# A depthwise 3x3 convolution moved to 64x64 TensorE tiles, with its later steps placed by a table

## The chip, the cores and the metric

The kernel runs on one core of one Trainium2 chip. The time is device microseconds of one execution, the median of several. The engines in the profile are PE (TensorE, matrix products), PEld (its weight loads), DVE (VectorE), ACT (ScalarE), POOL (GpSimd) and SP (SyncE, which starts transfers). All data are 32-bit floats, except for a few throw-away outputs.

## The reference, cut to what matters

The program is four residual layers over `x` of shape (4, 256, 48, 48). Each layer normalises its input in groups of 8 channels (`_gn`), computes something and adds it to `x`. Layer 0 is an 8-head attention, layer 1 a gate from a large depthwise convolution, layer 2 a one-head attention with a batch norm over all four images. The change is in layer 3:

```python
def _L3_conv_ref(x, attn_w1, attn_w2, refine_w, refine_b):
    p = jnp.mean(xw, axis=(2, 3))
    h = jax.nn.leaky_relu(p @ attn_w1.T, SLOPE)
    a = jax.nn.sigmoid(h @ attn_w2.T)
    y = xw * a[:, :, None, None]
    y = jax.lax.conv_general_dilated(y, refine_w, ..., feature_group_count=C)
    y = y + refine_b[None, :, None, None]
    mu = jnp.mean(y, axis=(2, 3), keepdims=True)
    var = jnp.mean(jnp.square(y - mu), axis=(2, 3), keepdims=True)
    y = (y - mu) * jax.lax.rsqrt(var + EPS)
    return jax.nn.leaky_relu(y, SLOPE)
x = x + _L3_conv_ref(_gn(x), ...)
```

So each channel is filtered by its own 3x3 kernel, gets a bias, is normalised over its 48x48 pixels, goes through a leaky ReLU and is added to `x`.

## The kernel before

Channels lie on the 128 partitions, in two halves `k`; pixels lie along the row, 2304 of them, cut into six slices of 384 (eight image rows). A tile of layer 3 is one image and one half of the channels, so there are eight (`TILES`). All engines follow an order written out by hand: each executes its instructions in the order in which the Python code emits them, and waits by semaphores for what the others make.

Layers 0 to 2 run in `attend`, a loop over attention groups into whose slots other work is placed. One such piece of work is `diagonals`, which lies beside the last attention of layer 2: for every tap that PE computes it builds a diagonal matrix of the tap's 128 weights, so that a product with it multiplies each channel by its own weight.

Layer 3 has a head, a loop and a tail. The head closes layer 2's batch norm (`sc2`, `bi2`), checks the softmax sums (`ok`, `okm`, `sound`, read at the very end to choose between this path and a general one), and prepares the first image: `Pre.first` multiplies by `Ww` on PE, ScalarE applies the batch norm, DVE or GpSimd add to `x`, `Pre.stats` and `Pre.chain` compute the group norm and the channel gate, and ScalarE writes the padded 50x50 images (`pads`). For the other images the same work is spread over the loop as `Pre.add`, `Pre.stats` and `Pre.chain`.

The loop runs over 8 tiles and, in each, over 6 slices. For each slice PE computes four of the nine taps (`PE_TAPS`) as 128x128 products into PSUM, one slice per bank (`products`). For each pair of slices DVE adds the five other taps, in place in PSUM, each reading a shifted window of the padded image (`taps`). Then ScalarE adds the bias, writes the result `z` to SBUF and sums it (`evict`). The steps that follow for each tile are `centre` and `square` (sum of squares about a rough mean, ScalarE), `scales` and `shift` (tiny DVE instructions and a GpSimd root), `scale` (ScalarE), `leak` (DVE), `gain` (add to `x`, GpSimd) and `store`. Their places are `if s == ...` lines in the loop, some a tile later, some two. `two_banks` hands out in turn the three PSUM tiles of two banks; a pair of slices takes one.

Of the kernel before, what the change touches and what calls it, by code (L numbers as in the profile page):

```python
# [9 lines left out]
F32 = mybir.dt.float32  # L10
AF = mybir.ActivationFunctionType
ALU = mybir.AluOpType
AX = mybir.AxisListType

P = 128
HW = 48
N = HW * HW
NK = 2
HEADS = 8
D = 64  # L20
NPAIR = HEADS // 2
JB = N // P
SL = 384
NSL = N // SL
# [13 lines left out]
V_BOUT, V_G1, V_B1, V_M1, V_V1, V_WB, V_G2, V_B2, V_RB = range(9)  # L38
# [31 lines left out]
LW = 2 * SL // P  # L70
SUM_HI = 1e25
SUM_LO = 1e-20


def usual_path(
    tc, x, wqkv, wout, vecs, dww, thphi_w, thphi_b, g_w, g_b, W_w, attn_w1, attn_w2, refine_w, out
):
    nc = tc.nc
# [12 lines left out]
    def pj_tile():  # L91
        return ps_pj.tile([P, 512], F32, tag="pj", name="pj")
# [16 lines left out]
    vec = cpool.tile([P, 9, NK], F32, name="vec")  # L109
# [18 lines left out]
    rfw = cpool.tile([P, NK, 9], F32, name="rfw")  # L128
# [5 lines left out]
    ident = cpool.tile([P, P], F32, name="ident")  # L134
# [12 lines left out]
    ones = cpool.tile([P, D], F32, name="ones")  # L147
# [6 lines left out]
    lsum = cpool.tile([P, LW], F32, name="lsum")  # L154
    nc.vector.memset(lsum, 0.0)
    lmin = cpool.tile([P, LW], F32, name="lmin")
# [70 lines left out]
    lp = main.enter_context(tc.tile_pool(name="l1", bufs=1))  # L227

    HALVES = (slice(0, D), slice(D, P))
# [383 lines left out]
    ident2 = lp.tile([P, D], F32, name="ident2")  # L613
# [394 lines left out]
        }  # L1008


    PE_TAPS = (0, 1, 2, 3)
    DVE_TAPS = (4, 5, 6, 7, 8)
    diag = {}

    def diagonals():

        for k in range(NK):
            xs = xsp.tile([P, NK, SL + 1], F32, tag="xs", name="diag")
            xs = xs.rearrange("p k s -> p (k s)")[:, : len(PE_TAPS) * P]
            diag[k] = xs.rearrange("p (t j) -> p t j", j=P)  # L1020
            for n, t in enumerate(PE_TAPS):
                nc.gpsimd.tensor_scalar(
                    diag[k][:, n, :], ident, rfw[:, k, t : t + 1], None, ALU.mult
                )
                yield 1

# [132 lines left out]
    n = NCH * NG  # L1159
    AT_CHUNK = AT_AFTER % NG  # L1160
    for i, (b, p) in enumerate(order):
# [12 lines left out]
        else:  # L1174
            start, slices = project2(0, norms2[0], twos[0])
# [9 lines left out]
        if b > 0:  # L1185
            end = n - 2 if (b, p) == (B - 1, NPAIR - 1) else n + 1
# [9 lines left out]
    n = L2C * NG  # L1196
    for b in range(B):
        work, others = {}, []

        def stats(b, c):  # L1200
            return [lambda k=k: w_stats(b, k, c) for k in range(NK)]
# [4 lines left out]
        if b + 1 < B:  # L1206
            spread(work, stats(b, 0), [22, 23])
            start, slices = project2(b + 1, norms2[b + 1], twos[b + 1])
# [6 lines left out]
            at = [s for s in range(n) if s in work or s % NG == AT_TOTAL]  # L1215
# [3 lines left out]
        else:  # L1219
            spread(work, stats(b, 0), [14, 15])  # L1220
            spread(work, stats(b, 1), [23, 24])
            others.append((diagonals(), NK * len(PE_TAPS), 4, 22))
        phases.append(([l2_unit(b, c, twos[b]) for c in range(L2C)], work, others))
# [34 lines left out]
    lp = l3.enter_context(tc.tile_pool(name="l3", bufs=1))  # L1258
    wk = l3.enter_context(tc.tile_pool(name="l3w", bufs=2))
# [20 lines left out]
    nc.vector.tensor_add(bi2, bi2, vec[:, V_B2, :])  # L1280


    W2 = HW + 2
    NPAD = 4
    pads = [lp.tile([P, W2, W2], F32, tag=f"pad{i}", name=f"pad{i}") for i in range(NPAD)]
    TILES = [(n, k) for n in range(B) for k in range(NK)]
    RS = SL // HW
    NG3 = NSL // 2
    GW = 2 * SL

    def two_banks(n):
        if n % 3 < 2:
            return sc_tile()
        return ps_av.tile([P, 2, 512], F32, tag="av", name="av3")
# [120 lines left out]
    class Conv:  # L1415


        def __init__(self, i):
            self.i, (n, self.k) = i, TILES[i]
            self.b = SEQ[n]  # L1420
            self.pad = pads[i % NPAD]
            self.z = big.tile([P, N], F32, tag="qk"[i // 2 % 2], name="z")

            self.st = small.tile([P, 2, NG3], F32, tag="in_st", name="in_st", bufs=3)
            self.ps = {}

        def products(self, s):
            g = s // 2
            if s % 2 == 0:
                self.ps[g] = two_banks(self.i * NG3 + g)  # L1430
            for n, t in enumerate(PE_TAPS):
                dr, dc = divmod(t, 3)
                nc.tensor.matmul(
                    self.ps[g][:, s % 2, :SL].rearrange("p (r c) -> p r c", c=HW),
                    lhsT=diag[self.k][:, n, :],
                    rhs=self.pad[:, s * RS + dr : (s + 1) * RS + dr, dc : dc + HW],
                    start=n == 0, stop=n == len(PE_TAPS) - 1,
                )

        def taps(self, g):  # L1440
            z = self.ps[g][:, :, :SL].rearrange("p h (r c) -> p h r c", c=HW)
            for t in DVE_TAPS:
                dr, dc = divmod(t, 3)
                r0 = 2 * g * RS + dr
                src = self.pad[:, r0 : r0 + 2 * RS, dc : dc + HW]
                nc.vector.scalar_tensor_tensor(  # L1446
                    z, src.rearrange("p (h r) c -> p h r c", h=2),
                    rfw[:, self.k, t : t + 1], z, ALU.mult, ALU.add,
                )

        def evict(self, g):
            nc.scalar.activation(
                self.z[:, g * GW : (g + 1) * GW].rearrange("p (h s) -> p h s", h=2),
                self.ps[g][:, :, :SL], AF.Identity, bias=vec[:, V_RB, self.k : self.k + 1],
                accum_out=self.st[:, 0, g : g + 1],
            )

        def centre(self):
# [45 lines left out]
    ALL = slice(0, N)  # L1504
    THIRDS = [slice(i * GW, (i + 1) * GW) for i in range(NG3)]
    for i in range(NPAD):
        for e in (0, W2 - 1):
            nc.gpsimd.memset(pads[i][:, e, :], 0.0)
            nc.gpsimd.memset(pads[i][:, 1 : W2 - 1, e : e + 1], 0.0)


    ok = lp.tile([P, 2, LW], F32, name="ok")
    nc.vector.tensor_scalar(ok[:, 0, :], lsum, SUM_HI, None, ALU.is_le)
    nc.vector.tensor_scalar(ok[:, 1, :], lmin, SUM_LO, None, ALU.is_ge)
    okm = lp.tile([P, 1], F32, name="okm")
    nc.vector.tensor_reduce(okm, ok, AX.XY, ALU.min)
    ps = pj_tile()
    nc.tensor.matmul(ps[0:1, 0:1], lhsT=okm, rhs=ones[:, 0:1], start=True, stop=True)
    sound = lp.tile([1, 1], mybir.dt.int32, name="sound")
    nc.vector.tensor_scalar(sound, ps[0:1, 0:1], P - 0.5, None, ALU.is_ge)  # L1520

    pres = {0: Pre(0), 1: Pre(1)}
    for i in range(NK * L2C):
# [12 lines left out]
            steps[NK * (b - 2) + 1, 2 * c] = (b, c)  # L1536
            steps[NK * (b - 1), 2 * c] = (b, L2C + c)

    convs, pending = [], None
    for i, (b, k) in enumerate(TILES):  # L1540
        cv = Conv(i)
        convs.append(cv)
        prev = convs[i - 1] if i else None
        older = convs[i - 2] if i > 1 else None
        final = i == len(TILES) - 1
        rest = iter(())
        for s in range(NSL):

            if pending:
                pending()  # L1550
                pending = None
            if s == 0 and k == 1 and b + 1 < B:
                rest = pres[b + 1].chain()
                next(rest)
            elif s:
                next(rest, None)
            step = steps.get((i, s))
            if step:
                n, at = step
                if n not in pres:  # L1560
                    pres[n] = Pre(n)
                pres[n].add(at)
                pending = lambda n=n, at=at: pres[n].stats(at)
            cv.products(s)
            next(rest, None)
            if s == 0 and prev:
                prev.taps(NG3 - 1)
                prev.evict(NG3 - 1)
            if s == 1 and prev:
                prev.square(NG3 - 1)  # L1570
                prev.scales()
            if s == 2:
                cv.taps(0)
                if prev:
                    prev.shift()
                cv.evict(0)
            if s == 3:
                cv.centre()
                if prev:
                    prev.scale(ALL)  # L1580
            if s == 4:
                cv.taps(1)
                cv.evict(1)
                cv.square(0)
            if s == 5:
                cv.square(1)
                if prev:
                    prev.leak(ALL)
            if older and s % 2:
                older.gain(THIRDS[s // 2], nc.gpsimd)  # L1590
                if s == NSL - 1:
                    older.store(ALL)
        _drain(rest)

    cv, prev = convs[-1], convs[-2]
    g = NG3 - 1
    cv.taps(g)
    cv.evict(g)
    cv.square(g)
    for cols in THIRDS:  # L1600
        prev.gain(cols, nc.gpsimd)
        prev.store(cols)
    cv.scales()
    cv.shift()
    for cols in THIRDS:
        cv.scale(cols)
        cv.leak(cols)
        cv.gain(cols, nc.vector)
        cv.store(cols)
    said = nc.values_load(sound[0:1, 0:1])  # L1610
    strict.close()
    l3.close()
# [843 lines left out]
```

## Time and profile before

| | |
|---|---|
| median time of 3 runs | 3713.06 us (3712.05 to 3713.46) |
| span of the profiled execution | 3710.8 us |
| PE busy | 3522.4 us (95%) |
| DVE busy | 2588.3 us (70%) |
| ACT busy | 2344.5 us (63%) |
| POOL busy | 1444.7 us (39%) |
| first convolution product of layer 3 | at 3480.92 us |
| L1446, the five taps on DVE | 120 instructions of 768 columns, 1.02 us each |
| L1433, the four taps on PE | 384 records of 384 columns |
| L1452, the eviction on ScalarE | 24 instructions, 0.90 us each |

Times inside the profile are microseconds from the start of the span. In a line of the timeline the first number is the start, the second the duration of the group; "x5" is a group of five instructions; the brackets tell how long the engine was idle before and on what it waited. In a table of windows each engine has its busy time and, in brackets, its number of instructions; PEclk is the share of the full TensorE clock that was granted. A product of 32-bit floats appears as two records.

### The profile page before, as it was taken

To read this page: it belongs to the slowest core of one execution; us is meant where nothing else is said; L and a number is where in the kernel's file an instruction comes from. 1 tells how busy PE (TensorE), PEld (TensorE's weight loads), DVE (VectorE), ACT (ScalarE), POOL (GpSimd) and SP (SyncE) were. 2 spreads that over 40 slices of the span, in tenths; PEclk is the share of its full clock that TensorE was granted. 3 is DMA by queue.
4 is the path that set the end of the run, shared out by engine and by line. 5 is a ranking of instruction groups with operands and counts; after the bars stand their busy time and mean duration, and the time that the engine had idled before them with its cause. 6 is when DMAs were issued, how large, how long until landed. Compare 5 with 4: busy or idle time off the path is not lost.

```text
span 3710.8 us, 86538 instructions
## 1 busy us (share of the span) xinstructions
PE 3522.4 (95%) x36330; PEld 1759.4 (47%) x36330; DVE 2588.3 (70%) x3203; ACT 2344.5 (63%) x3819; POOL 1444.7 (39%) x900
## 2 busy tenths in 40 slices
PE   7999999999999999999999999999999998999685
PEld 4444444454444444444444444444444445654343
DVE  2455555476778777967787779767968786576687
ACT  4665666666776677557766775587578555555353
POOL 2333333333334333433343334433433455664242
PEclk9999999999999999999999999999999999999797
DMA  4111111111111111121111111111111100000001
GB/s 138 24 25 21 26 21 26 21 25 21 25 21 26 20 29 17 34 55 34 21 25 21 25 21 25 21 25 21 25 16 25 17 6 6 6 8 4 26 29 74
DMA packets 114591, 97.89 MB, mean 26 GB/s; under 512 B 56224, under 2 KB 111632, under 8 KB 112400
## 3 DMA queue, kind: packets, MB, share of 16 engines
q1 hardware_dynamic: 111728, 91.27, 12.8%
q8 instruction: 286, 4.69, 0.5%
q10 hardware_dynamic: 2464, 1.00, 0.1%
q14 instruction: 113, 0.93, 0.1%
HBM read 59.33 MB, written 11.80 MB: 19 GB/s over the span
## 4 chain that ended last, share of the span: by engine, by line
PE 68%; DVE 18%; issue 5%; ACT 4%; POOL 3%; DMA 2%; SPq 0%; DVEq 0%; ACTq 0%; POOLq 0%
PE av L258 26%; PE sc L238 26%; DVE acc L284 7%; PE pj L512 6%; PE pj L584 3%; PE pj L533 3%; DVE sc L1446 2%; PE pj L291 1%; POOL half L269 1%; ACT pt L244 1%; DVE av L1446 1%; DVE acc L278 1%; PE pj L828 1%; ACT prod L766 1%; DMA xs<-in_x_dram 1%
## 5 line engine op out<-in xcount | busy, mean ns | idle before, releaser
L244 ACT ACTIVATE pt<-sc 128x768 f32<-128x768 f32 x1944 | 1476.5, 812 | 814.1 <-PE sc L238 805.4
L269 POOL TENSOR_TENSOR half<-pt 128x768 f32<-128x768 f32 x477 | 954.1, 2001 | 1673.4 <-ACT pt L244 1611.7
L238 PE MATMUL sc<-q,k 64*64 64x384 f32 x13824 | 1279.6, 485 | 12.7 <-ACT pt L244 9.9
L258 PE MATMUL av<-pt,v 64*64 64x384 f32 x13824 | 1279.8, 485 | 0.0
L284 DVE TENSOR_TENSOR acc<-acc,pt 128x768 f32<-128x768 f32 x792 | 930.7, 1175 | 86.2 <-DVE acc L284 1.8
L238 PEld LDWEIGHTS sc<-q,k 64*64 64x64 f32 x13824 | 510.6, 133 | 638.2 <-issue 499.9
L258 PEld LDWEIGHTS av<-pt,v 64*64 64x64 f32 x13824 | 514.4, 133 | 594.0 <-issue 557.3
L284 DVE TENSOR_TENSOR acc<-acc,half 128x768 f32<-128x768 f32 x459 | 468.6, 1021 | 335.7 <-POOL half L269 334.1
L589 DVE SCALAR_TENSOR_TENSOR x<-pj,bo,x 128x384 f32<-128x384 f32 x192 | 118.0, 615 | 461.9 <-PE pj L584 461.7
L512 PE MATMUL pj<-xs,w 128*128 128x384 f32 (+1 forms) x768 | 298.5, 512 | 3.2 <-issue 1.7
L766 ACT ACTIVATE prod<-pd,wt 128x256 f32<-128x256 f32 x486 | 280.6, 743 | 0.2
L339 POOL TENSOR_TENSOR o<-o,rinv 128x384 f32<-128x384 f32 x95 | 128.9, 1356 | 284.3 <-DMA rinv<-rinv 273.2
L512 PEld LDWEIGHTS pj<-xs,w 128*128 128x128 f32 x768 | 131.0, 190 | 157.3 <-issue 53.9
L584 PE MATMUL pj<-o,wo 128*128 128x384 f32 x384 | 159.8, 501 | 33.3 <-DVE x L589 28.7
L258 PE MATMUL av<-pt,qv 64*64 64x384 f32 x1728 | 173.9, 496 | 0.0
L238 PE MATMUL sc<-qv,kd 64*64 64x384 f32 x1728 | 169.4, 486 | 2.4 <-ACT pt L244 2.4
L784 DVE TENSOR_REDUCE prod<-prod 128x256 f32<-128x1280 f32 x114 | 168.5, 1478 | 0.0
L278 DVE TENSOR_TENSOR acc<-pt 128x768 f32<-128x768 f32 x99 | 139.3, 1407 | 26.4 <-ACT pt L244 26.4
L533 PEld LDWEIGHTS pj<-w,xs 128*128 128x128 f32 x1152 | 143.8, 192 | 26.0 <-issue 0.6
L533 PE MATMUL pj<-w,xs 128*128 128x128 f32 x1152 | 144.1, 275 | 0.0
L518 ACT ACTIVATE k<-pj,bias 128x384 f32<-128x384 f32 x96 | 55.7, 580 | 127.5 <-PE pj L512 127.0
L335 POOL TENSOR_TENSOR o<-raw 128x384 f32<-128x384 f32 x95 | 117.7, 1238 | 0.0
(226 smaller groups left out, 2686.7 us busy)
## 6 DMA issues: line engine op xcount, KB each, us to landing
xs<-in_x_dram SPq DMA_DIRECT2D x96, 384.0 KB
rinv<-rinv SPq DMA_DIRECT2D x208, 94.5 KB
x<-in_x_dram SPq DMA_DIRECT2D x6, 1152.0 KB
out_dram<-x SPq DMA_DIRECT2D x6, 1152.0 KB
l<-row SPq DMA_DIRECT2D x416, 1.5 KB
w<-in_wqkv_dram SPq DMA_DIRECT2D x32, 192.0 KB
rinv<-ls SPq DMA_DIRECT2D x208, 1.5 KB
x_out<-x SPq DMA_DIRECT2D x6, 384.0 KB
```

Source lines behind the costliest of these rows:

```text
L238: nc.tensor.matmul(ps[c * D : (c + 1) * D, h, :SL], lhsT=u["of"]["k"][r, j0 : j0 + D], rhs=u["of"]["q"][r, u["qc"]], start=True, stop=True,)
L244: nc.scalar.activation(pt, ps[:, :, :SL], AF.Exp, scale=u["scale"])
L258: nc.tensor.matmul(u["av"][h * D : (h + 1) * D, half, :SL], lhsT=value(u, j, h)[r], rhs=pt[r, h, :], start=j == 0, stop=j == JB - 1,)
L269: nc.gpsimd.tensor_add(half, pts[0], pts[1])
L278: nc.vector.tensor_add(u["acc"], ready[0], ready[1])
L284: nc.vector.tensor_add(u["acc"], u["acc"], term)
L339: eng.tensor_mul(o, o, u["rinv"])
L512: nc.tensor.matmul(ps[:, :n], lhsT=at["w"][:, k, t, :], rhs=xs[s][:, k, :n], start=k == 0, stop=k == NK - 1,)
L533: nc.tensor.matmul(ps[:, i * P : (i + 1) * P], lhsT=xs[s][:, k, i * P : (i + 1) * P], rhs=at["w"][:, k, 2, :], start=k == 0, stop=k == NK - 1,
L584: nc.tensor.matmul(ps[:, :SL], lhsT=wo[:, p, k * P : (k + 1) * P], rhs=o["o"], start=True, stop=True,)
L766: nc.scalar.activation(bufs[n % 3][:, :, min(n, 1) + i].rearrange("p (r c) -> p r c", c=AS), pd[:, PAD + dr : PAD + dr + AS, PAD + dc : PA ...
L784: nc.vector.tensor_reduce(to, bufs[n % 3][:, :, : min(n, 1) + len(taps)], AX.X, ALU.add)
```

## The change

Three things change. First, the products of layer 3 use 64x64 tiles of TensorE instead of the whole array: a diagonal matrix of 128 channels has only zeros in two of its four quadrants, so each half of the channels (`HALVES`, partitions 0 to 63 and 64 to 127) can be multiplied by itself, and the two other quadrants are free for another tap. Two taps are computed at a time for each half: the first (`e` = 0) goes to the same half of the output, the second (`e` = 1) to the other half. Eight of the nine taps thus go to TensorE.

Second, each half's sum is then in two places. `other` (ScalarE) brings the half that lies on the wrong partitions to the right ones in SBUF, `part`, and adds the bias, for which `rb_x` holds the bias with its halves exchanged. `own` (DVE) adds the ninth tap to the half that lies right and writes `z`. `join` (DVE) adds the two and sums the result. There is one PSUM tile of two banks for each slice now, instead of for each pair.

Third, the steps behind each slice are written as a table: `after` gives for each step its distance in slices from the tile's first and a rank within that slice, and `run` emits what is due. `scale`, `leak` and `gain` go by thirds of a tile. The check of the softmax sums becomes a generator, `judge`, that is advanced in the first tile's slices.

```diff
-    PE_TAPS = (0, 1, 2, 3)
-    DVE_TAPS = (4, 5, 6, 7, 8)
+    PE_TAPS, DVE_TAP = (0, 1, 2, 3, 5, 6, 7, 8), 4
...
-                    diag[k][:, n, :], ident, rfw[:, k, t : t + 1], None, ALU.mult
+                    diag[k][:, n, :], ident2, rfw[:, k, t : t + 1], None, ALU.mult
...
+    rb_x = lp.tile([P, NK], F32, name="rb_x")
+    for to, fr in zip(HALVES, HALVES[::-1]):
+        nc.sync.dma_start(rb_x[to, :], vecs[fr, V_RB, :])
...
         def products(self, s):
+            self.ps[s] = two_banks(self.i * NSL + s)
+            last = len(PE_TAPS) // 2 - 1
+            for n in range(last + 1):
+                for h, r in enumerate(HALVES):
+                    for e in range(2):
+                        nc.tensor.matmul(
+                            self.ps[s][HALVES[h ^ e], h, :SL].rearrange(
+                                "p (r c) -> p r c", c=HW
+                            ),
+                            lhsT=diag[self.k][r, 2 * n + e, :],
+                            rhs=self.window(r, s, PE_TAPS[2 * n + e]),
+                            start=n == 0, stop=n == last,
+                        )
+
+        def other(self, s):
...
+            for h, r in enumerate(HALVES):
+                fr = HALVES[1 - h]
+                nc.scalar.activation(
+                    self.part[g][r, s % 2, :], self.ps[s][fr, h, :SL], AF.Identity,
+                    bias=rb_x[fr, self.k : self.k + 1],
+                )
+
+        def own(self, s):
+            z = self.z[:, s * SL : (s + 1) * SL].rearrange("p (r c) -> p r c", c=HW)
+            for h, r in enumerate(HALVES):
                 nc.vector.scalar_tensor_tensor(
+                    z[r], self.window(r, s, DVE_TAP), rfw[r, self.k, DVE_TAP : DVE_TAP + 1],
+                    self.ps[s][r, h, :SL].rearrange("p (r c) -> p r c", c=HW),
+                    ALU.mult, ALU.add,
+                )
+
+        def join(self, g):
+            z = self.z[:, g * GW : (g + 1) * GW]
+            nc.vector.tensor_tensor_reduce(
+                z, z, self.part[g].rearrange("p h s -> p (h s)"), 1.0, 0.0, ALU.add, ALU.add,
+                self.st[:, 0, g : g + 1],
             )
...
+    def after(cv, final):
+        at = []
+        for s in range(NSL):
+            at += [(s + 1, 0, lambda s=s: cv.own(s)), (s + 1, 0, lambda s=s: cv.other(s))]
+        for g in range(NG3):
+            at.append((2 * g + 3, 1, lambda g=g: cv.join(g)))
+            at.append((2 * g + 4, 3, lambda g=g: cv.square(g)))
+        at.append((3, 1, cv.centre))
+        at += [(9, 2, cv.scales), (10, 2, cv.shift)]
+        eng = nc.vector if final else nc.gpsimd
+        for g, cols in enumerate(THIRDS):
+            at.append((10 + g, 4, lambda cols=cols: cv.scale(cols)))
+            at.append((11 + g, 1, lambda cols=cols: cv.leak(cols)))
+            at.append((12 + g, 5, lambda cols=cols: cv.gain(cols, eng)))
+            if final:
+                at.append((12 + g, 6, lambda cols=cols: cv.store(cols)))
+        if not final:
+            at.append((14, 6, lambda: cv.store(ALL)))
+        return at
```

More of the change, by code (lines that the diff above doesn't have):

```diff
@@ L1018, in diagonals @@
             xs = xsp.tile([P, NK, SL + 1], F32, tag="xs", name="diag")
-            xs = xs.rearrange("p k s -> p (k s)")[:, : len(PE_TAPS) * P]
-            diag[k] = xs.rearrange("p (t j) -> p t j", j=P)
+            xs = xs.rearrange("p k s -> p (k s)")[:, : len(PE_TAPS) * D]
+            diag[k] = xs.rearrange("p (t j) -> p t j", j=D)
             for n, t in enumerate(PE_TAPS):
                 nc.gpsimd.tensor_scalar(
-                    diag[k][:, n, :], ident, rfw[:, k, t : t + 1], None, ALU.mult
+                    diag[k][:, n, :], ident2, rfw[:, k, t : t + 1], None, ALU.mult
                 )
@@ L1424, in __init__, with window @@
             self.st = small.tile([P, 2, NG3], F32, tag="in_st", name="in_st", bufs=3)
-            self.ps = {}
+            self.ps, self.part = {}, {}
+        def window(self, r, s, t):
+            dr, dc = divmod(t, 3)
+            return self.pad[r, s * RS + dr : (s + 1) * RS + dr, dc : dc + HW]
         def products(self, s):
+            self.ps[s] = two_banks(self.i * NSL + s)
[11 more added lines that the diff above has]
+                        )
@@ L1428, in products @@
+        def other(self, s):
             g = s // 2
             if s % 2 == 0:
[L1430 to L1437, printed above, removed]
-                )
@@ L1440, in taps @@
[L1440 to L1445, printed above, removed]
+                self.part[g] = wk.tile([P, 2, SL], F32, tag="part", name="part")
+            for h, r in enumerate(HALVES):
[3 more added lines that the diff above has]
+                    bias=rb_x[fr, self.k : self.k + 1],
+                )
@@ L1446, in taps @@
+        def own(self, s):
+            z = self.z[:, s * SL : (s + 1) * SL].rearrange("p (r c) -> p r c", c=HW)
+            for h, r in enumerate(HALVES):
                 nc.vector.scalar_tensor_tensor(
-                    z, src.rearrange("p (h r) c -> p h r c", h=2),
-                    rfw[:, self.k, t : t + 1], z, ALU.mult, ALU.add,
-                )
[L1451 to L1455, printed above, removed]
+                    z[r], self.window(r, s, DVE_TAP), rfw[r, self.k, DVE_TAP : DVE_TAP + 1],
+                    self.ps[s][r, h, :SL].rearrange("p (r c) -> p r c", c=HW),
+                    ALU.mult, ALU.add,
+                )
@@ L1509, in usual_path, with judge @@
             nc.gpsimd.memset(pads[i][:, 1 : W2 - 1, e : e + 1], 0.0)
[L1512 to L1518, printed above, removed]
-    sound = lp.tile([1, 1], mybir.dt.int32, name="sound")
-    nc.vector.tensor_scalar(sound, ps[0:1, 0:1], P - 0.5, None, ALU.is_ge)
+    sound = lp.tile([1, 1], mybir.dt.int32, name="sound")
+    def judge():
+        ok = lp.tile([P, 2, LW], F32, name="ok")
+        nc.vector.tensor_scalar(ok[:, 0, :], lsum, SUM_HI, None, ALU.is_le)
+        nc.vector.tensor_scalar(ok[:, 1, :], lmin, SUM_LO, None, ALU.is_ge)
+        okm = lp.tile([P, 1], F32, name="okm")
+        nc.vector.tensor_reduce(okm, ok, AX.XY, ALU.min)
+        yield
+        ps = pj_tile()
+        nc.tensor.matmul(ps[0:1, 0:1], lhsT=okm, rhs=ones[:, 0:1], start=True, stop=True)
+        yield
+        nc.vector.tensor_scalar(sound, ps[0:1, 0:1], P - 0.5, None, ALU.is_ge)
+        yield
     pres = {0: Pre(0), 1: Pre(1)}
@@ L1537, in usual_path, with run @@
             steps[NK * (b - 1), 2 * c] = (b, L2C + c)
-    convs, pending = [], None
+    def after(cv, final):
[17 more added lines that the diff above has]
+        return at
+    events = {}
+    def run(t, ranks):
+        now = [(rank, fn) for rank, fn in events.get(t, ()) if rank in ranks]
+        for _, fn in sorted(now, key=lambda job: job[0]):
+            fn()
+    pending, verdict = None, judge()
     for i, (b, k) in enumerate(TILES):
         cv = Conv(i)
[L1542 to L1545, printed above, removed]
+        for dt, rank, fn in after(cv, i == len(TILES) - 1):
+            events.setdefault(i * NSL + dt, []).append((rank, fn))
         rest = iter(())
         for s in range(NSL):
+            t = i * NSL + s
+            run(t, (0,))
             if pending:
@@ L1565, in usual_path @@
             next(rest, None)
[L1566 to L1592, printed above, removed]
-        _drain(rest)
[L1595 to L1609, printed above, removed]
+            if i == 0:
+                next(verdict, None)
+            run(t, range(1, 7))
+        _drain(rest)
+    end = len(TILES) * NSL
+    for t in range(end, end + 9):
+        run(t, range(7))
     said = nc.values_load(sound[0:1, 0:1])
```

## The prediction

> **What bounds the kernel now.** I read the page first and then asked the trace about the last 260 us, where the edited code runs. Part 2 of the page shows PE at 9 tenths for 36 of 40 slices; only the last three slices, layer 3, look different. The windows over layer 3 (head, loop of convolution slices, tail) give its size and its busiest engine:
>
> ```profile
> core 0: us, PE busy (x) PEld busy (x) DVE busy (x) ACT busy (x) POOL busy (x), PEclk, DMA share, GB/s
> 3454.00:3481.00 27.00, 10.96 (x74) 5.42 (x71) 14.95 (x43) 8.55 (x9) 8.10 (x21) 0.63 0.07 30
> 3481.00:3695.00 214.00, 168.26 (x556) 87.05 (x556) 174.78 (x258) 97.61 (x145) 75.42 (x49) 0.88 0.09 37
> 3695.00:3711.00 16.00, 0.00 (x0) 0.00 (x0) 6.59 (x12) 4.88 (x7) 0.73 (x2) 0.50 0.28 108
> ```
>
> The loop is 214 us for 8 tiles, 26.8 us each. DVE is busy 82% of it, PE 79% at a clock of 0.88. The chain of waits inside the loop says which of the two is the limit:
>
> ```profile
> by line: DVE sc L1446 26.3%; DVE av L1446 15.3%; DVE z L1495 9.0%; PE sc L1433 7.6%; issue 7.0%; ACT z L1452 4.5%; DVE gn_st L1345 3.6%; ACT junk L1465 3.3%; POOL x L1340 3.2%; ACT pad L1408 2.0%; ACT tmp L1316 2.0%; POOL x_back L1340 1.6%;
> ```
>
> DVE's taps (L1446) and leak (L1495) are half of it; PE's products only 7.6%. The timeline of a late tile shows the mechanism: five taps run one after another in 5.25 us, ScalarE's eviction waits 6.29 us for them, and PE's next products wait for the eviction.
>
> ```profile
> 3653.25 5.25 DVE L1446 SCALAR_TENSOR_TENSOR sc<-pad,rfw,sc 128x768 f32<-128x768 f32 x5
> ...
> 3658.59 0.90 ACT L1452 ACTIVATE z<-sc,vec 128x768 f32<-128x768 f32 x1 [6.29 <-DVE sc L1446]
> ...
> 3659.63 4.81 PEld L1433 LDWEIGHTS sc<-pad,diag 128*128 128x128 f32 x16 [0.94 <-ACT z L1452]
> 3659.63 5.43 PE L1433 MATMUL sc<-pad,diag 128*128 128x384 f32 x16 [0.33 <-ACT z L1452]
> ```
>
> So layer 3 is bound by DVE, and PE's four taps per slice cost 5.43/2 = 2.7 us per slice (x16 are two slices; an f32 product leaves two records).
>
> [...] The trace agrees with the very order that the change uses (row half outside, column half inside): layer 1's L828 does 48 records of 256 columns in 2.66 us up to the next product, 12 rounds of 0.22 us, so four tiles at once; the attention's 16 records of 384 columns take 1.29 us, 4 rounds of 0.32. [...] the one-element in_mr (L1485) takes 0.15 us alone and up to 1.57 us when a GpSimd add is running, leak up to 3.23 against a median of 2.55. [...]
>
> ```profile
> 3190.39 2.86 PE L828 MATMUL pj<-pd,diag 64*64 64x256 f32 x48
> 3193.05 1.50 PE L258 MATMUL av<-pt,qv 64*64 64x384 f32 x16
> ...
> L950 ACT ACTIVATE kd<-pj,bias 64x384 f32<-64x384 f32 x24 | 13.8, 575 | 15.0 <-PE pj L944 14.7
> ```
>
> **The change part by part.** I sum each engine's work over the loop of 48 slices, because in-order engines with three two-bank buffers average out over slices, then add what the sum leaves out.
>
> PE. Per slice 16 products, 32 records, 8 rounds of 0.3225 = 2.58 us, about the same as now, for eight taps. 48 x 2.58 = 123.8. The 18 later `add` steps are two rounds each, 0.65: 11.7. Three chains with about 2 us of tiny matmuls and idle time: 6. Cold clock at the first products: 5.46 us for 8 records where 16 take 5.43 when warm, 2.7 more. Sum 144.
>
> DVE. Removed: 120 taps of 768 columns at a pitch of 1.055 (126.6 us). Added: `own`, 96 of 64x384. A 128x384 instruction of the same kind (L589) takes 0.618; partitions don't count, and with the pitch gap of the taps (1.055 - 1.023) it is 0.65: 62.9. If the two halves overlapped as L1345's pairs do (547 ns each, 1.02 for two) it would be 0.54: 52. I take 62.9. `join`, 24 of 768: the plain DVE add of that shape is 0.96; with reading out the accumulator, for which ScalarE pays 0.19, 1.15. [...] 23 of them lie in the loop: 26.5. Leak in thirds is 0.96 each, 19 in the loop: 18.2 (now 2.55 a tile). Unchanged: stats 18 x 1.02 = 18.4, tiny instructions of `scales`/`shift`/`centre` 9.5, chains 7.5, the moved check 1. Sum 144.
>
> ScalarE. Removed: 24 evictions of 0.90 + 0.19 with their 85 us of waits for DVE (50.3 and 34.5). Added: `other`, 96 of 64x384 at L950's 0.575 plus a gap, 0.59: 56.6. Squares 24 x 1.06 = 25.4, scale in thirds 21 x 0.95 = 20, `tmp` 18 x 1.21 = 21.8, pads 7 x 2.31 = 16.2. Sum 140. The exchange between halves is free of extra work here: L836 already reads one half and writes the other.
>
> GpSimd. Adds and gains are unchanged, 42 x 1.82, with the roots 81 us; half of the new loop. Sixteen 64-wide diagonals instead of eight 128-wide (L1022, 0.60 to 1.41 us each) lie in the last attention unit, where GpSimd waits 2.4 to 10.6 us for ScalarE before its adds: nothing.
>
> So three engines stand at 144, 144 and 140. What is left over is DVE's contention with GpSimd. Before, 24 exposed places (two groups of small instructions and one leak per tile) lost 8 x (0.90 - 0.15) + 7 x (2.66 - 2.55), about 7 us, 0.28 each at a GpSimd share of 75/214 = 0.35. After, 64 places (three joins, three leaks, two groups per tile) at a share near 81/165 = 0.49 lose 0.28 x 0.49/0.35 = 0.40 each: 25 us. A few fall where DVE would wait for PE anyway; I take 21. Loop: 144 + 21 = 165 us against 214.
>
> The table of distances places `join` two slices after its last product, `square` one later, `scales` one after that. By then each input is ready in the slice before, so the waits it adds (own on products, other on products, join on other) are absorbed by the buffers. Behind a waiting `own` on DVE stand the stats and the chain, for which PE waits only in tiles 1, 3 and 5, already counted.
>
> Head. `judge` leaves the path: now DVE's L1513 to L1516 and a matmul (3458.0 to 3459.2) stand before the first products on PE, and ScalarE's first eviction starts at 3460.92. Without it the products follow the last statistics' at 3454 and the eviction starts when bi2 is ready, 3458.1: 2.7 us less. The two tiny rb_x loads have 25 us to land.
>
> Tail. From the last product: own 1.3, two leaks of the tile before 1.9, join 1.15, square 1.05, scales 1.15, waits 0.7, then as now from the root to the end (3698.1 to 3710.8) 12.7. Sum 20, against 16.
>
> Total: 2.7 + (214 - 165) - 4 = 47.7 us less: 3713.1 - 47.7 = **3665 us**.
>
> **Rivals.** (a) Contention hides in idle time and the loop runs at PE's rate, 148, tail 19: another 17 us off, 3648. For: DVE's sum alone is no more than PE's. [...] (c) Products run two tiles at a time, since two successive ones share a row half: 5.16 a slice, 248 + 20 = 268 us of PE, 103 more than my loop: 3768, slower. Against: L828. (d) `own` halves overlap and DVE drops by 10 us: near (a).
>
> **How the numbers follow.** Main case 0.55, (a) with (d) 0.22, (b) 0.17, (c) 0.05; 0.01 for a new dependency stall that eats exactly the gain. The range 3642 to 3690 takes in (a) and (b) with a few us each side. Faster 0.94, same 0.01, slower 0.05.
>
> **What would show it.** Right: PE records 64*64 for the conv with 32 per slice in 2.6 us and PEclk near 1 in the loop; own near 0.62 us, other 0.575, join near 1.15; DVE over 85% busy in the loop with joins and leaks stretched beside GpSimd adds; first eviction of the head near 3458. Wrong: join near 2 us, products in steps of 0.64 us per round, or ScalarE as the releaser that PE waits for most.

## The result, and the profile after

The changed kernel takes 3714.83 us (median, 3711.97 to 3715.81) beside 3712.56 us for the kernel before on the same chip: a ratio of 1.0005, interval 0.9987 to 1.0022. No change that can be measured, where 3665 us was forecast.

The windows over head, loop and tail of the profiled execution (span 3714.1 us; 3710.8 before):

```profile
core 0: us, PE busy (x) PEld busy (x) DVE busy (x) ACT busy (x) POOL busy (x), PEclk, DMA share, GB/s
3454.00:3478.00 24.00, 9.25 (x48) 4.20 (x44) 14.55 (x42) 7.67 (x8) 8.08 (x21) 0.57 0.10 40
3478.00:3691.00 213.00, 172.09 (x1710) 79.62 (x1710) 134.40 (x288) 130.60 (x202) 75.61 (x46) 0.89 0.09 35
3691.00:3714.00 23.00, 0.00 (x0) 0.00 (x0) 12.61 (x21) 9.36 (x14) 7.25 (x4) 0.53 0.26 106
```

VectorE's work has fallen and ScalarE's has grown, as planned: 134 and 131 us. But the loop is still 213 us long, so each of them is idle for over a third of it. From first to last product the loop takes 211 us (200 before), and what follows the last product 24 us (30 before).

The groups of instructions in the loop of the changed kernel (busy time, mean ns of one, then idle time before it and its releaser):

```profile
L1440 PE MATMUL sc<-pad,diag 64*64 64x384 f32 x1024 | 111.4, 547 | 6.7 <-ACT part L1456 3.5 <-ACT pad L1411 1.7 <-issue 1.5
L1465 DVE SCALAR_TENSOR_TENSOR z<-pad,rfw,sc 64x384 f32<-64x384 f32 x64 | 39.2, 613 | 20.8 <-PE sc L1440 19.8
L1456 ACT ACTIVATE part<-sc,rb_x 64x384 f32<-64x384 f32 x62 | 35.7, 576 | 57.9 <-DVE z L1465 52.6 <-PE pj L1312 4.6
L1473 DVE CUSTOM_DVE_ANT_0 z<-z,part 128x768 f32<-128x768 f32 x22 | 25.4, 1157 | 0.1
L1473 DVE DVE_READ_ACCUMULATOR2_ANT in_st<- 128x1 f32 x22 | 1.8, 80 | 0.0
```

The durations are those of the forecast: `own` (L1465) 613 ns, `other` (L1456) 576 ns, `join` (L1473) with its read-out 1.24 us in the mean, where 1.15 was forecast. What the forecast does not have is the third row's last column. The list of waits (what waits, for what, us in total, times, longest) has it at the top:

```profile
ACT part L1456 <- DVE z L1465: 70.8, 28, 5.6
POOL x L1343 <- ACT tmp L1319: 50.8, 12, 8.9
```

ScalarE's `other` waits 70.8 us for VectorE's `own`. No data passes between the two: they read different partitions of the products and write different tiles. The chain of waits over the loop spreads over every line, with no engine in the lead:

```profile
by line: issue 16.9%; PE sc L1440 12.1%; DVE z L1465 10.5%; DVE z L1473 9.1%; PE av L1440 7.2%; ACT part L1456 5.7%; PE pj L1312 4.7%; DVE z L1515 4.5%; POOL x L1343 4.3%; ACT tmp L1319 3.7%; POOL x_back L1343 3.4%; DVE gn_st L1348 2.9%; AC
```

The timeline of one added step (start, us, engine, line; the wait in brackets) shows what that means:

```profile
3544.05 4.30 POOL L1519 TENSOR_TENSOR x<-x,z 128x768 f32<-128x768 f32 x2
3544.13 1.02 DVE L1348 BATCH_NORM_STATS2 gn_st<-x 128x6 f32<-128x384 f32 x2 [2.19 <-POOL x L1343]
3545.06 1.62 DVE L1515 SCALAR_TENSOR_TENSOR z<-z 128x768 f32<-128x768 f32 x1
3545.26 3.01 PE L1440 MATMUL sc<-pad,diag 64*64 64x384 f32 x32
3546.61 2.57 DVE L1473 CUSTOM_DVE_ANT_0 z<-z,part 128x768 f32<-128x768 f32 x1
...
3549.19 1.24 DVE L1465 SCALAR_TENSOR_TENSOR z<-pad,rfw,sc 64x384 f32<-64x384 f32 x2
...
3550.53 1.17 ACT L1456 ACTIVATE part<-sc,rb_x 64x384 f32<-64x384 f32 x2 [5.32 <-DVE z L1465]
3551.72 1.23 ACT L1319 ACTIVATE tmp<-pj,bi,sc 128x384 f32<-128x384 f32 x2
3552.45 1.48 PE L1312 MATMUL pj<-y,Ww 64*64 64x384 f32 x5 [4.17 <-ACT tmp L1319]
```

VectorE waits 2.19 us for GpSimd, then does statistics, leak, join and own one after another, two of them stretched beside GpSimd's adds: 1.62 us for leak and 2.57 for join, where with no add beside them neither took more than 0.96 in this profile. All that time ScalarE stands before `other` (5.32 us), and behind `other` in its queue stands `tmp`, for which TensorE's next added products wait 4.17 us. The engines take turns instead of working side by side.

The last tiles have no adds and still show it, here in tile 6. ScalarE's `scale` (L1511) comes first, then VectorE's `leak` (L1515), which has waited for it, `join` (L1473) and `own`, and only then ScalarE's `other`, after 2.03 us of waiting:

```profile
3661.84 1.01 ACT L1511 ACTIVATE z<-z,in_mr,in_ri 128x768 f32<-128x768 f32 x1
...
3662.88 0.96 DVE L1515 SCALAR_TENSOR_TENSOR z<-z 128x768 f32<-128x768 f32 x1 [0.77 <-ACT z L1511]
3663.76 0.95 DVE L1473 CUSTOM_DVE_ANT_0 z<-z,part 128x768 f32<-128x768 f32 x1
...
3664.73 1.24 DVE L1465 SCALAR_TENSOR_TENSOR z<-pad,rfw,sc 64x384 f32<-64x384 f32 x2
...
3666.07 1.16 ACT L1456 ACTIVATE part<-sc,rb_x 64x384 f32<-64x384 f32 x2 [2.03 <-DVE z L1465]
```

### The profile page after: what moved, and what is told of

It reads as the page before. It is cut to its first block, busy times and chain, and to the rows that moved or that the text cites. A ratio compares the mean times of both kernels' runs of the same rounds, so it can differ in the third digit from the quotient of the medians.

```text
span 3714.1 us, 89018 instructions
## 1 busy us (share of the span) xinstructions
PE 3527.9 (95%) x37482; PEld 1749.9 (47%) x37482; DVE 2551.6 (69%) x3241; ACT 2382.2 (64%) x3881; POOL 1458.1 (39%) x908
## 4 chain that ended last, share of the span: by engine, by line
PE 69%; DVE 15%; issue 6%; ACT 4%; POOL 3%; DMA 2%; SPq 0%; DVEq 0%; ACTq 0%; POOLq 0%
PE av L258 26%; PE sc L238 26%; DVE acc L284 6%; PE pj L512 6%; PE pj L584 3%; PE pj L533 3%; POOL half L269 2%; PE pj L291 1%; ACT pt L244 1%; DMA rinv<-rinv 1%; DVE acc L278 1%; ACT prod L766 1%; PE pj L828 1%; PE sc L1440 1%; DVE z L1465 1%
## 5 line engine op out<-in xcount | busy, mean ns | idle before, releaser
L589 DVE SCALAR_TENSOR_TENSOR x<-pj,bo,x 128x384 f32<-128x384 f32 x192 | 118.0, 615 | 458.4 <-PE pj L584 458.1
L584 PE MATMUL pj<-o,wo 128*128 128x384 f32 x384 | 158.7, 498 | 33.0 <-DVE x L589 28.4
L1440 PE MATMUL sc<-pad,diag 64*64 64x384 f32 x1024 | 111.4, 547 | 6.7 <-ACT part L1456 3.5
```

The costliest lines, as they stand in the source:

```text
L584: nc.tensor.matmul(ps[:, :SL], lhsT=wo[:, p, k * P : (k + 1) * P], rhs=o["o"], start=True, stop=True,)
L1440: nc.tensor.matmul(self.ps[s][HALVES[h ^ e], h, :SL].rearrange("p (r c) -> p r c", c=HW), lhsT=diag[self.k][r, 2 * n + e, :], rhs=self.win ...
```

## The experiments

Medians are in us; ratios are against the kernel before on the same chip, with 95% intervals. The changed kernel itself stands at 3714.83. Nearly all edits are in the table of distances, `after`.

**Four first runs.** My first theory was a ring through GpSimd's adds and VectorE's statistics. `e1_other_first` emits `other` before `own`; `e2_stats_late` has the statistics of an added step come one slice later; `e4_both` does both; `e3_no_adds` leaves the added steps of the loop out.

```diff
# e1, e4
-at += [(s + 1, 0, lambda s=s: cv.own(s)), (s + 1, 0, lambda s=s: cv.other(s))]
+at += [(s + 1, 0, lambda s=s: cv.other(s)), (s + 1, 0, lambda s=s: cv.own(s))]
# e2, e4
-pending = lambda n=n, at=at: pres[n].stats(at)
+late = 1 if t == NSL - 1 else 2
+pending.setdefault(t + late, []).append(lambda n=n, at=at: pres[n].stats(at))
# e3
-pres[n].add(at)
```

> Theory A (ring): other waits for own because both read the same PSUM bank; own stands in DVE's queue behind the stats, which wait for GpSimd's add, which waits for ScalarE's tmp, which stands behind other. Emitting other before own cuts that ring, since ScalarE then waits for PE alone: tiles 0 to 5 fall from 29 us to 20 to 23 us each, time 3670 to 3695 us, and ScalarE's wait for own (71 us) is gone. Rival B (clock): the loss is PE's half clock after gaps and feeds itself; the order of two reads moves less than 8 us. Rival C: the wait only changes sides, own now waits for other on DVE as long as other waited for own: within 8 us.

> Stats of an added slice one slice later (not for the last of tile 0). Theory A: the ring is cut at GpSimd's add instead; DVE's 23 us of waiting for GpSimd vanish and own starts earlier: 3675 to 3700 us. Rival B: within 8 us. Rival C: within 8 us, since other still waits for own.

> The loop's add steps (product with Ww, batch norm on ScalarE, add to x on GpSimd) are left out for images 2 to 4 of the order; stats and chain stay. Theory A: no ring is left; tiles 0, 2 and 4 go to about 17 us, tiles 1, 3 and 5 to about 22: 45 to 60 us less than the changed kernel, about 3655 to 3670 us. Rival B: only PE's own share of 12 us and a little, about 3700 us.

> Both edits. Theory A: about the better of the two alone, a few us less: 3665 to 3690 us. If each cuts a different wait the gains add up. Rival B: within 10 us of the changed kernel.

Measured: e1 3717.73 (1.0014, 1.0007 to 1.0021), e2 3712.9 (0.9998, 0.9988 to 1.0008), e4 3718.19 (1.0013, 1.0006 to 1.0020). The ring theory falls: in e2 VectorE's 22.8 us of waiting for GpSimd are gone, but its wait at `leak` grows from 9.3 to 19.4 us and the time stays. e3 takes 3673.47 (0.9895, 0.9866 to 0.9924), 3 us above the ring theory's range: the adds cost some 41 us in the loop, but that includes all their work. And without any add, `other` still waits 51.1 us for `own` in e3. The useful line is in e1's list of waits:

```profile
DVE z L1465 <- ACT part L1456: 74.6, 23, 8.8
```

The order is turned round, and so is the wait, as rival C had it: 70.8 us of ScalarE for VectorE became 74.6 us of VectorE for ScalarE. So the two reads of one slice's products are held in the order of the program, whichever it is. That gave the next theory: this order makes the engines take turns.

**e5 and e9: `other` one slice later.** Then it never meets `own` of its own slice.

```diff
-(s + 1, 0, lambda s=s: cv.other(s))     +(s + 2, 0, lambda s=s: cv.other(s))
-(2 * g + 3, 1, ... cv.join(g))          +(2 * g + 4, 1, ... cv.join(g))
-(2 * g + 4, 3, ... cv.square(g))        +(2 * g + 5, 3, ... cv.square(g))
-(9, 2, cv.scales), (10, 2, cv.shift)    +(10, 2, cv.scales), (11, 2, cv.shift)
-(10 + g, 4, ... cv.scale(cols))         +(11 + g, 4, ... cv.scale(cols))
-(11 + g, 1, ... cv.leak(cols))          +(13 + g, 1, ... cv.leak(cols))    # e9: 12 + g
# gain and store move along with leak
```

> ScalarE's other moves one slice back (s + 2), join, square, scales and scale one slice with it, leak and gain two; all work stays. Theory R (round trip: own and other of a slice use the same two PSUM banks and are put in program order, and the table then sends the slice back and forth between VectorE and ScalarE, one of them idle while the other works): other no longer stands behind own of its own slice, the 71 us that ScalarE waits for own fall under 20, the period of two slices in the last tile falls from 6.35 us to near PE's 5.2, and the loop loses 25 to 45 us: 3670 to 3690. Rival A (the ring through ScalarE's tmp, GpSimd's add and PE's pj tiles of the added steps sets tiles 0 to 5): only tiles 6 and 7 gain, some 5 us: 3708. Rival P (TensorE's cold clock alone, no wait): no change, 3715.

> The table of e5, with leak one slice behind scale again as in the changed kernel: the only edit is that other comes one slice later and everything behind it moves by the same one slice. If the program order of own and other at one bank is the cause, nearly all of e5's gain stays: 3685 to 3692. If e5 owed its gain to leak's second slice of distance: 3700 to 3712.

e5 takes 3686.71 (0.9932, 0.9916 to 0.9949), e9, where everything behind `other` moves by the same one slice, 3682.44 (0.9918, 0.9901 to 0.9934): 28 and 32 us less than the change, with all the work still there. e5 lies in its range; e9 is 3 us faster than its own. The 6.35 us of tile 6 that e5's expectation names are no good measure of the turn-taking: TensorE itself took 6.90 us for two slices there (3657.74 to 3664.64), the first of them at a lowered clock (shown further down). In e9 the wait of `other` for `own` inside the loop falls to:

```profile
ACT part L1456 <- DVE z L1465: 4.0, 9, 1.3
```

and its windows show a loop of 177 us with about the same busy time of VectorE and ScalarE:

```profile
3478.00:3655.00 177.00, 157.14 (x1710) 73.76 (x1702) 138.84 (x289) 130.50 (x201) 79.25 (x46) 0.94 0.10 42
```

The timeline of e9 has both at work at once and TensorE at its own pace (x48 are a slice and a half):

```profile
3639.16 4.05 PE L1440 MATMUL sc<-pad,diag 64*64 64x384 f32 x48
3639.40 1.24 DVE L1465 SCALAR_TENSOR_TENSOR z<-pad,rfw,av 64x384 f32<-64x384 f32 x2 [0.37 <-PE av L1440]
3640.13 1.16 ACT L1456 ACTIVATE part<-sc,rb_x 64x384 f32<-64x384 f32 x2
3640.68 0.96 DVE L1515 SCALAR_TENSOR_TENSOR z<-z 128x768 f32<-128x768 f32 x1
```

Tile 7 has neither adds nor a chain, and the full clock in both kernels. From its first product to its last, in the changed kernel and then in e9:

```profile
3672.50:3690.10 17.60, 16.41 (x196) 6.79 (x188) 14.28 (x28) 13.11 (x23) 7.30 (x4) 1.00 0.17 70
3639.20:3654.80 15.60, 15.60 (x196) 7.13 (x188) 14.70 (x28) 12.93 (x22) 7.30 (x4) 1.00 0.19 78
```

TensorE is idle for 1.2 us of it in the changed kernel and never in e9.

**e7: a wider table alone.** `own` and `other` stay together; join comes one slice later, square, scales and scale two, leak and gain three.

```diff
-(2 * g + 3, 1, ... cv.join(g))          +(2 * g + 4, 1, ... cv.join(g))
-(2 * g + 4, 3, ... cv.square(g))        +(2 * g + 6, 3, ... cv.square(g))
-(9, 2, cv.scales), (10, 2, cv.shift)    +(11, 2, cv.scales), (12, 2, cv.shift)
-(10 + g, 4, ... cv.scale(cols))         +(12 + g, 4, ... cv.scale(cols))
-(11 + g, 1, ... cv.leak(cols))          +(14 + g, 1, ... cv.leak(cols))
```

> own and other stay together one slice behind; join one slice later, square, scales and scale two, leak and gain three; same work. Rival T (the table's distances of one slice make join, square and leak wait for the other engine within the slice): 20 to 40 us faster, 3675 to 3695. Theory R with the bank order as the main part: own to other stays, under 10 us: 3705 to 3715.

3697.91 (0.9960, 0.9945 to 0.9974), 17 us less than the change: more than the bank-order theory allowed, less than the rival's lower figure. The tight distances are part of the cause. VectorE's wait at `leak` falls from 14.2 us over the whole kernel to 2.2 (`join` waited for nothing in either kernel), so `own` is done earlier. The wait of `other` for it falls from 70.8 to 52.8 us, by about as much as the time.

**e6 and e8: the halves interleaved.** I took the order to be one of banks, and let the engines start on different banks.

```diff
-at += [(s + 1, 0, lambda s=s: cv.own(s)), (s + 1, 0, lambda s=s: cv.other(s))]
+at.append((s + 1, 0, lambda s=s: cv.both(s)))  # own(s, 0), other(s, 1), own(s, 1), other(s, 0)
```

> own of half 0, other from half 1's bank, own of half 1, other from half 0's bank, in this order in each slice; same work, same distances. If the order of reads in the same bank is what holds ScalarE (theory R's first half), other waits at most 0.6 us a slice in place of about 1.3, and the time falls by some 0.6 x 48 = 29 us at most: 3685 to 3700. If the tight distances of the table are the cause (rival T), the wait moves to join and leak and the time stays within 5 us: 3710 to 3716.

> e6's interleaved halves, e7's wider table and the statistics of an added step one slice later, together. Theory R and rival T both: the fastest of the four, 3665 to 3685, with VectorE and ScalarE over 75% busy in the loop. Rivals A and P: 3700 to 3715.

e6 takes 3740.19 (1.0077, 1.0061 to 1.0094), 25 us more than the change; e8, which adds it to e7's table and e2's later statistics, 3721.61 (1.0023, 1.0013 to 1.0033), 24 us more than e7. Both expectations missed. The timeline of one slice of e6 says why:

```profile
3671.12 0.61 DVE L1468 SCALAR_TENSOR_TENSOR z<-pad,rfw,av 64x384 f32<-64x384 f32 x1
3671.76 0.57 ACT L1460 ACTIVATE part<-av,rb_x 64x384 f32<-64x384 f32 x1 [0.88 <-DVE z L1468]
3672.37 0.62 DVE L1468 SCALAR_TENSOR_TENSOR z<-pad,rfw,av 64x384 f32<-64x384 f32 x1 [0.64 <-ACT part L1460]
3673.02 0.58 ACT L1460 ACTIVATE part<-av,rb_x 64x384 f32<-64x384 f32 x1 [0.69 <-DVE z L1468]
```

The first two of these instructions read different banks, and still the second starts only when the first has ended. All four stand in a row. What orders them may be the tile, which holds both banks; the next runs test that.

**e13, e14, e15: a tile for each bank.** The six banks of layer 3 become six one-bank buffers; the orders are the change's, e6's and e9's.

```diff
-return ps_av.tile([P, 2, 512], F32, tag="av", name="av3")    # or sc_tile()
+return [ps_bk.tile([P, 512], F32, tag="bk", name="bk") for _ in range(2)]
-self.ps[s][r, h, :SL]       +self.ps[s][h][r, :SL]
```

> The changed kernel's order and distances, with each slice's two banks as two tiles of their own (six one-bank buffers in place of three of two banks; the head's normalisation takes two instructions for one). If the order holds over a whole tile (theory W), other of half 0 may now start when own of half 0 is done, so that half of the serial stretch goes: some 0.6 us a slice, 15 to 25 us faster than the change, 3690 to 3702. If the order holds by bank (theory B), nothing changes, since the changed kernel then already had it: 3712 to 3718.

> e13 with e6's interleaved order. Theory W: own of half 0 runs beside other from half 1's bank and the reverse, nothing serial is left in a slice; what cost 25 us in e6 now gains: 3680 to 3692, and the waits of own for other (44 us in e6) fall under 10. Theory B: as e6, 3735 to 3745.

> e9 with two one-bank tiles per slice. Own and other of one slice no longer meet in e9, so finer buffers have little to free: within 4 us of e9's 3682 (3679 to 3687), up to 1 us of it for the head's extra instructions. If buffers coming free late were part of what is left: 3670 to 3678.

e13 takes 3704.5 (0.9979, 0.9972 to 0.9986), 10 us less than the change: outside what an order by bank allows, though less than the 15 to 25 expected. Its timeline shows the difference directly:

```profile
3659.97 1.26 DVE L1467 SCALAR_TENSOR_TENSOR z<-pad,rfw,bk 64x384 f32<-64x384 f32 x2
...
3660.62 1.23 ACT L1458 ACTIVATE part<-bk,rb_x 64x384 f32<-64x384 f32 x2 [1.19 <-DVE z L1467]
```

`other` starts when the first of the two `own` instructions is done and runs beside the second; in the lines of the changed kernel above it starts after both. e14 takes 3711.73 (0.9998, 0.9989 to 1.0007), 28 us less than e6 for the same order of instructions. So the order goes by tile. But e14 missed its own figure of 3680 to 3692, and `own` still waits 40.0 us for `other`. Each bank now has its own hand-over, one in each direction, and whichever engine is late at one of them may still hold up the other; no run tests this reading. e15 takes 3681.13 (0.9921, 0.9904 to 0.9938), the same as e9: once a slice lies between the two reads, finer tiles have nothing left to free.

**e10, e11, e12: the chain of an image.** e9 still misses the forecast by 17 us. Start of the first products of a tile to those of the next, us:

| tile | 0 | 1 | 2 | 3 | 4 | 5 | 6 | 7 |
|---|---|---|---|---|---|---|---|---|
| before | 30.3 | 28.4 | 21.2 | 30.9 | 17.8 | 34.2 | 16.0 | 21.2 |
| after | 28.9 | 28.4 | 26.5 | 38.1 | 24.7 | 27.2 | 20.0 | 17.5 |
| e9 | 25.3 | 26.8 | 19.4 | 29.7 | 18.8 | 25.3 | 16.4 | 15.7 |
| e5 | 26.0 | 26.8 | 18.7 | 31.6 | 18.1 | 26.9 | 17.2 | 17.2 |
| e12 | 26.0 | 19.3 | 18.7 | 24.4 | 19.0 | 23.1 | 16.4 | 16.8 |

In e9, tiles 1, 3 and 5, which hold the chain of the next image, take 25 to 30 us, tiles 2, 4, 6 and 7 take 16 to 19; tile 0, with an add in each slice, takes 25. e10 is e5 with two empty turns ahead of the chain's first matmul, e11 has e2's later statistics too, e12 is e5 without the chain of images two to four.

```diff
# e10, e11: in chain(), ahead of the first matmul
+yield
+yield
# e12: in chain()
+if self.n:
+    for _ in range(8):
+        yield
+    yield from self.padded(*pres[0].factors)
+    return
```

> e5, with the chain's first matmul one slice further behind its aggregation (two empty turns), so that TensorE does not stand at it. The trace of e5 has tiles 1, 3 and 5 (which hold a chain) at 26.8, 31.6 and 26.9 us and tiles 2, 4, 6, 7 at 17 to 19. If the chain's wait at its first matmul, and the cold clock after it, are the remaining loss, these three tiles fall by 4 to 8 us each: 3665 to 3677. If the later pads then hold back the next tile instead: 3683 to 3690.

> e10 with the statistics of an added step one slice later too. VectorE no longer stands before a statistic that waits for GpSimd's add; tile 0, with an add in each slice, gains most: 3 to 8 us under e10. If VectorE's wait there is only room it has anyway: equal to e10 within 2 us.

> e5 with the chain of images two to four left out: their pads are scaled with the first image's factors; adds, statistics and all convolutions stay. It prices the chain: my prediction had 6 us for TensorE's part in all three. If that price was right: 3678 to 3682. If the chain's waits are the rest of the loss, tiles 1, 3 and 5 come down to the 18 to 19 us of tiles 2 and 4: 3660 to 3668.

e12 takes 3669.84 (0.9887, 0.9870 to 0.9903), 17 us less than e5 and between its two expectations: tile 1 comes down to 19.3 us as expected, tiles 3 and 5 only to 24.4 and 23.1. The 17 us are the price of the three chains, where the forecast has 6 in TensorE's sum (and 7.5 in VectorE's). TensorE waits at three of their four groups of matmuls (in e5's loop 8.6, 1.5 and 2.8 us). The timeline of e9 at tile 5 shows where it is paid:

```profile
3600.48 1.02 DVE L1348 BATCH_NORM_STATS2 gn_st<-x_back 128x6 f32<-128x384 f32 x2
...
3601.59 1.24 DVE L1465 SCALAR_TENSOR_TENSOR z<-pad,rfw,av 64x384 f32<-64x384 f32 x2
...
3602.86 0.49 DVE L1356 BATCH_NORM_AGGREGATE gn_mv<-gn_st 128x2 f32<-128x36 f32 x2
...
3603.50 0.35 PE L1359 MATMUL pj<-gn_mv,gmat 128*128 128x2 f32 x2 [3.24 <-DVE gn_mv L1356]
```

TensorE stands 3.24 us at a matmul of 0.35 us, because the aggregation is queued on VectorE behind the statistics and two `own`. e10, which moves that matmul back, takes 3695.43 (0.9957, 0.9940 to 0.9973), 9 us more than e5, and e11 3695.5 (0.9950, 0.9934 to 0.9967): a miss. In e10 TensorE no longer waits at that matmul, but the pads come later, and the next tile's first products wait 10.3 us for them, in three places (3.10 us at tile 2). So it is the chain's length that counts, not the place of one matmul in it.

## Why the prediction was wrong

**The step that failed** is the one behind all sums: "in-order engines with three two-bank buffers average out over slices", with "the waits it adds (own on products, other on products, join on other) are absorbed by the buffers". The list leaves one wait out, `other` on `own`, since no data passes there. That wait was 70.8 us long, and it closes a circle: VectorE's `own` stands in its queue behind `leak`, which waits for ScalarE's `scale`, and ScalarE's `other` waits for `own`, with the next `scale` behind it. Here three buffers did not absorb a wait between two readers of the same buffer. Moving `other` by one slice gave back 32 us of the 50 that were missing (e9), with nothing else removed. Widening the other steps of the circle alone gave 17 (e7). A sign of being wrong that the forecast names came true as well: of the named releasers, ScalarE is the one that L1440 waits for most, 13.0 us for `other` and 4.0 for the pads.

**Terms that were mis-sized.** The chains: "three chains with about 2 us of tiny matmuls and idle time: 6" has work and waiting together; in e5 TensorE works 5.2 us for them and waits 12.9. The clock: the forecast has 2.7 us for cold first products and expects a clock near 1 after them. TensorE is busy 172.1 us in the changed kernel's loop, where the forecast's whole sum for it is 144; e9 still has 157.1. The windows above bound what the clock itself can have cost, as an estimate: a share of 0.11 withheld over 213 us is 23 us of full clock at most, 0.06 over e9's 177 us is 11. The difference is some 13 us, where e9 gains 32. The kernel before stood no better, with 0.90 over the 200 us from its first to its last product. One pause of the changed kernel shows a fall of the clock behind a wait (PEclk is the third number from the end):

```profile
3653.00:3655.40 2.40, 2.33 (x32) 0.81 (x24) 0.00 (x0) 2.40 (x3) 0.00 (x0) 1.00 0.00 0
3655.40:3657.70 2.30, 0.00 (x0) 0.00 (x0) 1.17 (x2) 2.25 (x5) 0.13 (x1) 1.00 0.00 0
3657.70:3662.00 4.30, 4.26 (x32) 1.92 (x36) 4.19 (x7) 3.27 (x6) 3.41 (x2) 0.60 0.00 0
```

After 2.41 us without products the clock is 0.60 in the mean and the slice takes 4.50 us, where the next one, at the full clock, takes 2.58 (3662.06 to 3664.64, from its first product to that of the slice behind it). Finer windows give 1.00 up to 3658.40, 0.50 from 3658.42 to 3661.80, and 1.00 again from 3661.85. So the fall came some 0.7 us after the products had begun again at 3657.74; what sets its moment was not shown. How much of the loss is the clock's own, within the bound above, and how much comes with the waits, no run here separates. The contention with GpSimd: 21 us were taken; `join` lost 4.5 us over 24 (1140 ns in the mean against a median of 951), `leak` about 2, and `in_mr`, which took up to 1.57 us in the kernel before, nothing (0.16 us at most). The tail took 24 us, not 20.

**What was right.** TensorE's slice: 2.58 us warm for eight taps. `own` 0.613 on 64 partitions, where L589 took 0.618 on 128. Two of them take 1.24, so the two halves do not overlap, which had been an estimate of the author's; rival (d) falls. `other` 0.576. `join` 0.951 with a read-out of 0.080, not near the 2 us that the forecast names; rival (b), a slower `join`, which no trace had shown, falls. Rival (c) falls with TensorE's rate. Rival (a), TensorE's rate as the limit, is what tile 7 of e9 shows: 15.7 us for 6 slices, 2.6 each. The head: pads begin at 3476.23, where before it was 3478.46, 2.2 us of the 2.7. The case that came, a new stall that eats the gain, stood in the forecast at one in a hundred.

From first product to end the forecast was 165 + 20 = 185 us. Measured: 230 before, 235 after, 201 in e9, and 189 in e12, which leaves the chains out, so that its coming near confirms nothing. The forecast sets its 165 and 20 us, which part at the last product, against 214 and 16 of the kernel before, which part at 3695 us. Parted at the last product these are 200 and 30; the sum of 230 is the same. Two of its readings are loose without bearing on the sums: TensorE is at 9 tenths in 35 slices of the page, not 36, and the chain of waits that it calls the loop's takes in the tail.

**What stays open.** Whether the wait of `other` for `own` could simply be dropped. `own` and `other` of one bank read different halves of the partitions, but no run here took the wait away in place, so it was not shown.

The kernel to keep is e9 (3682.44) or e15 (3681.13), both 0.8% faster than the kernel before; between them the runs do not decide.

## What to carry to other kernels

Before summing engines' work into a forecast, list every pair of engines that touches one buffer, readers too, and ask in which order the program puts them: two readers of one tile may be run one after the other though no data passes, as here (70.8 us of waits). Where both lie in the same step of a software pipeline, put a step between them (32 us less in e9); a table of distances makes that one number. When work falls on every engine and the time does not, look for the wait at the top of the list and for what stands behind it in the queue, not for the busiest engine.

## What the runs showed that was not expected

- The order of two reads held over a whole two-bank tile: reads of different banks by ScalarE and VectorE ran one after another in 0.61 + 0.57 + 0.62 + 0.58 us (e6), and giving each bank its own tile took 28 us off the same instructions (e14).
- Finer hand-overs within one tile cost more than a coarse one: three per slice instead of one made the kernel 25 us slower (e6).
- An added wait that one would think local travels: 5.32 us of ScalarE before `other` became 4.17 us of TensorE before products of quite another part, by way of the queue.
